# Attention key masks in quarters of the array's rows, those of two score groups together

## Chip, cores and metric

The kernel runs on one core of a Trainium2 chip. The core has a matrix engine (TensorE, PE in the profile, with its weight loads shown apart as PEld), a vector engine (DVE), a scalar engine (ACT), a general engine (POOL) and a queue engine (SP) that issues most transfers. The metric is the device time of one execution in microseconds; the figure used is the median of several runs.

## The reference

The reference is an attention layer followed by a mixture-of-experts feed-forward layer, added to the input. The attention has 16 sequences of 512 tokens and 16 heads of width 64, with one key and value shared by all heads, an additive bias per head, a causal mask and a key mask per sequence. The part that matters here, shortened:

```python
q = (xn @ Wq).reshape(b, n, H, DH).transpose(0, 2, 1, 3) * scale
sim = jnp.einsum('bhid,bjd->bhij', q, k)
sim = sim + bias
sim = jnp.where(causal_mask, neg, sim)
...
sim = jnp.where(mask_p[:, None, None, :], sim, neg)
attn = jax.nn.softmax(sim, axis=-1)
out = jnp.einsum('bhij,bjd->bhid', attn, v)
```

The key mask hides keys of a sequence from all its queries and heads. After attention come a projection, a layer norm, and a layer of 16 experts in which each expert picks its 512 best tokens.

## The kernel before

The attention stage runs over 16 sequences x 8 head pairs = 128 pairs, in one loop over `p` (line 630). A pair is two heads, and its work is spread over several rounds of the loop: in round `p` the scores of pair `p` are computed and reduced, the queries of pair `p + 1` are projected, the probabilities of the pair behind are transposed in squares by DVE and moved by transfers, and the pair behind that one is multiplied with the values (`attend`). Beside this run the output projection of the sequence before (`project`), norms, and the preparation of the sequence after (`turn`, `keys_values`, `turn_values`, `mask`). The order on each engine is the order in which the program is written: the wrapper `Pinned` (line 119) keeps it. Transfers on SP are placed by the scheduler.

The scores of a pair are causal, so the query block `q` of 128 rows has 128 (q + 1) keys: 512, 384, 256 and 128 columns for blocks 3, 2, 1 and 0. They go to PSUM in three groups: block 3, then blocks 2 and 0 in one bank, then block 1. Each group takes two tiles, one for each head, of the pool `ps_s`, which has four. `scores` (line 425) writes them. The two heads of the pair lie in the two halves of the array's 128 rows: head 0 in rows 0 to 63, head 1 in rows 64 to 127, with keys `ka` and queries `qa` laid out accordingly, so that their matmuls run beside each other.

The key mask is added by a matmul of its own ahead of each score product, into the same PSUM tile: the stationary operand `one_sb` is zero but for one row of ones in each half (lines 189 to 192), and the moving operand `km` has, in that row, 0 for a key that counts and -2^100 for one that doesn't. Both are bf16; the score product is fp32. In each call the order is mask, product, mask, product:

```python
te.matmul(
    sps[j][:, at : at + w], one_sb[halves[j], :], sq.km[halves[j], :w],
    start=True, stop=False,
)
```

`mask` (line 270) fills `km` once for each sequence: for each half it loads the 512 mask bytes into a row of `m8` over SP, and DVE converts that row into the row of `km`. There are two `km` tiles, used in turn.

After the scores, `reduce` (line 449) on DVE adds the bias and takes each row's extreme, and frees the PSUM tiles; `exps` on ACT follows. The body of the loop (lines 645 to 670) calls `scores(3)`, `scores(2, 0)`, the reductions of blocks 3, 2 and 0, then two of the four steps of the next pair's queries (half of them), `scores(1)`, the rest of the queries, and the reduction of block 1.

Of the kernel before, what the change touches and what calls it, by code (L numbers as in the profile page):

```python
# [8 lines left out]
F32 = mybir.dt.float32  # L9
# [3 lines left out]
U8 = mybir.dt.uint8  # L13
# [6 lines left out]
P = 128  # L20
# [6 lines left out]
def tile_adaln_ffn(  # L27
# [21 lines left out]
    nc = tc.nc  # L49
    B, N, D = x.shape  # L50
    H = 2 * bias.shape[0]
    DH = null_kv.shape[1]
    E, _, F = fc1.shape
# [14 lines left out]
    ext = [P * (q + 1) for q in range(QB)]  # L68
# [60 lines left out]
    te, ve, se, ge = [Pinned(a) for a in (nc.tensor, nc.vector, nc.scalar, nc.gpsimd)]  # L129


    with ExitStack() as st:
# [3 lines left out]
        small = st.enter_context(tc.tile_pool(name="small", bufs=4))  # L136
# [7 lines left out]
        ps_s = st.enter_context(tc.tile_pool(name="ps_s", bufs=4, space=PSUM))  # L144
# [41 lines left out]
        mhalf = const.tile([P, 1], F32, name="mhalf")  # L186
        nc.vector.memset(mhalf, -0.5)

        one_sb = const.tile([P, P], BF16, name="one_sb")
        nc.vector.memset(one_sb, 0.0)  # L190
        for j in range(2):
            nc.vector.memset(one_sb[j * DH : j * DH + 1, :], 1.0)
        kms = []
        for i in range(2):
            km = const.tile([P, N], BF16, name=f"km{i}")
# [31 lines left out]
        def load_bias(p):  # L227


            bt = biasp.tile([P, 2, SW], F32, name=f"bias_{p}", tag="bias")  # L230
            if p >= HP:
                nc.sync.dma_start(out=bt, in_=causal[p % HP])
                return bt
            nc.sync.dma_start(out=bt, in_=bias[p])
            for q in range(QB):
                diag = bt[:, :, off[q] + ext[q] - P : off[q] + ext[q]]
                ge.affine_select(
                    out=diag, in_=diag, pattern=[[0, 2], [-1, P]],
                    compare_op=ALU.is_ge, fill=-BIG, base=0, channel_multiplier=1,
                )  # L240
            nc.sync.dma_start(out=causal[p], in_=bt)
            return bt

        class Sequence:
# [23 lines left out]
                )  # L268

            def mask(self):  # L270
                m8 = small.tile([DH + 1, N], U8, name=f"m8_{self.b}", tag="m8", bufs=1)
                self.km = kms[self.b % 2]
                for r in (0, DH):
                    nc.sync.dma_start(out=m8[r : r + 1, :], in_=mask[self.b : self.b + 1, :])
                for r in (0, DH):
                    ve.tensor_scalar(
                        self.km[r : r + 1, :], m8[r : r + 1, :], BIG, -BIG, ALU.mult, ALU.add
                    )
# [125 lines left out]
        class Pair:  # L404
# [17 lines left out]
                self.qa = qap.tile([P, N], F32, name=f"qa_{self.name}", tag="qa")  # L422
                se.activation(self.qa, qp, AF.Copy, scale=scale)

            def scores(self, *blocks):

                sq = self.sq
                sps = [
                    ps_s.tile([P, N], F32, name=f"sp_{self.name}_{j}_{blocks[0]}", tag="s")
                    for j in range(2)  # L430
                ]
                halves = [slice(j * DH, (j + 1) * DH) for j in range(2)]
                at = 0
                for q in blocks:
                    w = ext[q]
                    for j in range(2):
                        te.matmul(
                            sps[j][:, at : at + w], one_sb[halves[j], :], sq.km[halves[j], :w],
                            start=True, stop=False,
                        )  # L440
                    for j in range(2):
                        te.matmul(
                            sps[j][:, at : at + w], self.qa[halves[j], q * P : (q + 1) * P],
                            sq.ka[halves[j], :w], start=False, stop=True,
                        )
                    self.sps[q] = [sps[j][:, at : at + w] for j in range(2)]
                    at += w

            def reduce(self, q, bias_t):

# [105 lines left out]
        def steps(*parts):  # L556
            for part in parts:
                if hasattr(part, "__next__"):
                    yield from part
                else:  # L560
                    part()
                yield

        def some(todo, n=None):

            while n is None or n > 0:
                if next(todo, todo) is todo:
                    return
                n = None if n is None else n - 1
# [7 lines left out]
        halves, norms, routes, first, ins, loads = {}, {}, {}, {}, {}, {}  # L577
        early = HP - 3
        for b in range(B):
            at = b * HP  # L580
# [48 lines left out]
        now, behind, turned, late = None, None, None, ()  # L629
        for p in range(B * HP + 1):  # L630
            b, hp = divmod(p, HP)
            now, ahead = ahead, None
            if p + 1 < B * HP:
                biases[p + 1] = load_bias(p + 1)
                ahead = Pair(seqs[(p + 1) // HP], (p + 1) % HP)
            for c, t in loads.get(p, ()):
                seqs[c].load(t)
            bt = biases.pop(p, None)
            chains = [InNorm(seqs[c], t) for c, t in ins.get(p, ())]
            if p in norms:  # L640
                chains.append(OutNorm(seqs[norms[p][0]], norms[p][1]))
            second = steps(*[seqs[c].project(*divmod(h, 2)) for c, h in halves.get(p, ())])
            asked = ahead.queries() if ahead else steps()

            if now:
                now.scores(3)
                now.scores(2, 0)
                now.reduce(3, bt)
                now.exps(3)
                now.reduce(2, bt)  # L650
                now.reduce(0, bt)
                now.exps(2)
                now.exps(0)
            for n in late:
                n.root()
            if now and behind:
                behind.turn()
                behind.move(nc.sync, range(6, SN * SN))
                behind.move(ge, range(6))
            for n in late:  # L660
                n.d()
            some(asked, 1)
            if now:
                now.scores(1)
            else:
                behind.turn_last()
            some(asked)
            if now:
                now.reduce(1, bt)
                now.exps(1)  # L670
            some(second, 1)
            if p in routes:
                seqs[routes[p][0]].turn_router(routes[p][1])
            for n in chains:
                n.a()
            if now:
                now.sums()
            if turned:
                turned.attend()
            for n in chains:  # L680
                n.b()
            if now:
                now.normalize(0)
                now.normalize(3)
            for part in first.get(p, ()):
                part()
            if now:
                now.normalize(2, 1)
            some(second, 2)
            if p in routes:  # L690
                seqs[routes[p][0]].logits(routes[p][1])
            some(second)
            for n in chains:
                n.c()
            late = chains
            for t in {HP - 2: (0,), HP - 1: (1,), HP: (2, 3)}.get(p - end * HP, ()):
                seqs[end].project_part(t, range(early))
            if not now:
                behind.attend()
            turned, behind = behind, now  # L700
# [64 lines left out]
    te, ve, ge = [Pinned(a) for a in (nc.tensor, nc.vector, nc.gpsimd)]  # L765
# [49 lines left out]
    with ExitStack() as st:  # L815
# [107 lines left out]
        groups = []  # L923
# [253 lines left out]
    now = Expert(0, first)  # L1177
# [11 lines left out]
    for e in range(E):  # L1189
# [72 lines left out]
        now = nxt  # L1262
# [53 lines left out]
```

## Time and profile before

| | us |
|---|---|
| median of 3 runs | 3651.52 |
| lowest, highest | 3649.92, 3652.57 |
| the profiled execution | 3655.35 |
| its span in the profile | 3653.6 |
| score products, x2048, first and last start | 50.2 to 1898.1 |
| mask products, x1024, first and last start | 49.5 to 1897.8 |

The profiled execution's span starts with its first and ends with its last recorded instruction, so the execution is 1.75 us longer than it. Attention fills a little over half of the span; the experts follow. In the profile, `sp<-km,one_sb` is a mask product, `sp<-ka,qa` a score product, `qp` a query projection, `op` an output projection, `ap` the product with the values, `xfp` a transpose or a router product, and `p<-sp,bias,nn_sb` on DVE a reduction. Nearly all are recorded at line 127, that of the wrapper, so they are told apart by their tiles. A shape such as 64*128 ahead of the operand sizes is the part of the array that a matmul uses, rows by columns. A time in a line of the timeline is the start of the first instruction in it, and the next number is how long the line's instructions lasted together; matmuls overlap, so the distance between starts tells what one costs.

### The profile page before, as it was taken

To read this page: it belongs to the slowest core of one execution; us is meant where nothing else is said; L and a number is where in the kernel's file an instruction comes from. 1 tells how busy PE (TensorE), PEld (TensorE's weight loads), DVE (VectorE), ACT (ScalarE), POOL (GpSimd) and SP (SyncE) were. 2 spreads that over 40 slices of the span, in tenths; PEclk is the share of its full clock that TensorE was granted. 3 is DMA by queue.
4 is the path that set the end of the run, shared out by engine and by line. 5 is a ranking of instruction groups with operands and counts; after the bars stand their busy time and mean duration, and the time that the engine had idled before them with its cause. 6 is when DMAs were issued, how large, how long until landed. Compare 5 with 4: busy or idle time off the path is not lost.

```text
span 3653.6 us, 52226 instructions
## 1 busy us (share of the span) xinstructions
PE 3441.1 (94%) x16972; PEld 2478.7 (68%) x16972; DVE 2330.9 (64%) x6028; ACT 1585.2 (43%) x4152; POOL 894.3 (24%) x1314
## 2 busy tenths in 40 slices
PE   5799999999999999999993699999999999999998
PEld 2355556555565555555552488888888888888887
DVE  4567676777667767767656865555565666555553
ACT  3567676676666766667660111111121111111111
POOL 2232332332332323233320222111121122222110
PEclk9799999999999999999996799999999999999999
DMA  7777666676667676676642233333333334333330
GB/s 251 241 212 225 207 205 209 211 221 214 203 208 222 213 212 205 205 214 198 196 148 104 70 118 110 104 93 94 115 122 119 119 122 122 110 122 110 112 91 12
DMA packets 263286, 583.58 MB, mean 160 GB/s; under 512 B 49255, under 2 KB 118023, under 8 KB 245607
## 3 DMA queue, kind: packets, MB, share of 16 engines
q1 hardware_dynamic: 215680, 473.44, 39.0%
q0 software_dynamic: 42960, 101.29, 12.3%
q10 hardware_dynamic: 4375, 5.53, 0.4%
q8 instruction: 136, 2.23, 0.3%
q14 instruction: 135, 1.11, 0.1%
HBM read 349.64 MB, written 61.87 MB: 113 GB/s over the span
## 4 chain that ended last, share of the span: by engine, by line
PE 50%; DVE 5%; issue 1%; DMA 1%; POOL 0%; ACT 0%; SPq 0%; DVEq 0%; POOLq 0%; ACTq 0%
PE r_y L127 9%; PE pc L127 6%; PE pc_y L127 6%; PE pa_y L127 6%; PE pa L127 6%; PE pe L127 3%; PE pb L127 3%; PE pd L127 3%; PE op L127 2%; PE qp L127 2%; PE sp L127 1%; PE ap L127 1%; DVE sel L836 1%; PE xgp L127 1%; DVE sq L127 1%
## 5 line engine op out<-in xcount | busy, mean ns | idle before, releaser
L127 ACT ACTIVATE p<-p,nm 128x512 f32<-128x512 f32 (+3 forms) x1024 | 561.9, 550 | 243.8 <-DVE nm L127 242.5
L127 DVE CUSTOM_DVE_ANT_0 p<-sp,bias,nn_sb 128x512 f32<-128x512 f32 (+3 forms) x1024 | 500.5, 546 | 174.1 <-PE sp L127 174.0
L127 POOL DMA_DIRECT2D pt<-sq x762 | 381.6, 508 | 877.6 <-issue 559.8
L127 PE MATMUL qp<-xnt,wq_sb 128*128 128x512 f32 x1024 | 512.2, 623 | 0.0
L127 PE MATMUL op<-wo_sb,ot 128*128 128x256 f32 x1920 | 457.0, 382 | 8.8 <-ACT ot L127 8.6
L127 PEld LDWEIGHTS op<-wo_sb,ot 128*128 128x128 f32 x1920 | 357.4, 190 | 109.3 <-issue 54.3
L127 DVE STREAM_TRANSPOSE sq<-p 128x896 f32<-128x896 f32 x762 | 398.7, 589 | 49.8 <-DMA pt<-sq 27.5
L127 ACT ACTIVATE p<-p,rs 128x512 f32<-128x512 f32 (+2 forms) x768 | 406.2, 603 | 1.9 <-DVE rs L127 1.1
L127 POOL DMA_INDIRECT out_dram<-y,tok x64 | 106.2, 1659 | 1184.3 <-ACT y L1145 1184.3
L1053 ACT ACTIVATE h<-h,b_sb 128x512 f32<-128x512 f32 (+1 forms) x256 | 143.4, 607 | 529.1 <-DVE h L127 471.1
L127 PE MATMUL sp<-ka,qa 64*128 64x512 f32 (+3 forms) x2048 | 357.7, 440 | 1.8 <-ACT qa L127 1.8
L127 PE MATMUL ap<-pt,vp 128*64 128x512 f32 (+3 forms) x2048 | 310.8, 446 | 18.6 <-DMA pt<-sq 9.1
L1145 ACT ACTIVATE y<-y,gg 128x512 f32<-128x512 f32 x64 | 46.2, 722 | 647.3 <-DVE y L127 647.3
L127 PEld LDWEIGHTS qp<-xnt,wq_sb 128*128 128x128 f32 x1024 | 174.9, 190 | 183.2 <-issue 167.8
L127 PEld LDWEIGHTS ap<-pt,vp 128*64 128x64 f32 x2048 | 148.8, 139 | 195.4 <-issue 158.1
L127 PE MATMUL pa<-xe,w 128*128 128x256 f32 x1024 | 243.5, 381 | 0.0
L127 PEld LDWEIGHTS sp<-ka,qa 64*128 64x128 f32 x2048 | 174.2, 190 | 87.5 <-issue 81.5
L127 PE MATMUL pa_y<-w,h 128*128 128x256 f32 x1024 | 231.5, 379 | 0.0
L127 PE MATMUL r_y<-w2t,hs 128*128 128x256 f32 x1024 | 231.5, 379 | 0.0
L127 PEld LDWEIGHTS pa<-xe,w 128*128 128x128 f32 x1024 | 195.9, 191 | 27.0
L127 PEld LDWEIGHTS r_y<-w2t,hs 128*128 128x128 f32 x1024 | 194.6, 190 | 26.5
L127 PEld LDWEIGHTS pa_y<-w,h 128*128 128x128 f32 x1024 | 193.4, 190 | 25.7
(191 smaller groups left out, 5191.6 us busy)
## 6 DMA issues: line engine op xcount, KB each, us to landing
bias<-causal SPq DMA_DIRECT2D x120, 1280.0 KB
w<-in_fc_dram SPq DMA_DIRECT2D x256, 512.0 KB
pt<-sq SPq DMA_DIRECT2D x1270, 80.0 KB
pt<-sq POOLq DMA_DIRECT2D x762, 80.0 KB
x<-in_x_dram SPq DMA_DIRECT2D x64, 256.0 KB
out_dram<-x SPq DMA_DIRECT2D x64, 256.0 KB
table<-xf SPq DMA_DIRECT2D x64, 256.0 KB
bias<-in_bias_dram SPq DMA_DIRECT2D x8, 1280.0 KB
```

Source lines behind the costliest of these rows:

```text
L127: return lambda *args, **kwargs: tc.keep_in_program_order(made(*args, **kwargs))
L836: nc.vector.tensor_scalar(flags, l2, than, None, op, ALU.add, accum_out=red)
L1053: nc.scalar.activation(a[0], a[1], AF.Gelu, bias=b1_sb[:, self.e, f : f + 1])
L1145: nc.scalar.activation(y, y, AF.Copy, scale=self.gg[:, g, self.e : self.e + 1])
```

## The change

The rows of ones and masks stand in four quarters of 32 rows instead of two halves: rows 0, 32, 64 and 96. `mask` loads and converts four rows for each sequence instead of two. `scores` takes groups of blocks. It first writes the masks of all the groups it is given, group 0 in the first quarter of each head's half and group 1 in the second, 32 rows each, and then all the score products, which are 64 rows as before. Blocks 3 and (2, 0) now go together in one call as two groups; block 1 is a call of its own with one group. The flag that clears a bank stands only on the first mask in each bank.

```diff
+        MR = P // 4
         one_sb = const.tile([P, P], BF16, name="one_sb")
         nc.vector.memset(one_sb, 0.0)
-        for j in range(2):
-            nc.vector.memset(one_sb[j * DH : j * DH + 1, :], 1.0)
+        for r in range(0, P, MR):
+            nc.vector.memset(one_sb[r : r + 1, :], 1.0)
...
             def mask(self):
-                m8 = small.tile([DH + 1, N], U8, name=f"m8_{self.b}", tag="m8", bufs=1)
+                m8 = small.tile([P, N], U8, name=f"m8_{self.b}", tag="m8", bufs=1)
                 self.km = kms[self.b % 2]
-                for r in (0, DH):
+                for r in range(0, P, MR):
                     nc.sync.dma_start(out=m8[r : r + 1, :], in_=mask[self.b : self.b + 1, :])
-                for r in (0, DH):
+                for r in range(0, P, MR):
                     ve.tensor_scalar(
                         self.km[r : r + 1, :], m8[r : r + 1, :], BIG, -BIG, ALU.mult, ALU.add
                     )
...
-            def scores(self, *blocks):
+            def scores(self, *groups):
...
+                for g, blocks in enumerate(groups):
+                    sps = [
+                        ps_s.tile([P, N], F32, name=f"sp_{self.name}_{j}_{blocks[0]}", tag="s")
+                        for j in range(2)
+                    ]
+                    at = 0
+                    for q in blocks:
+                        self.sps[q] = [sps[j][:, at : at + ext[q]] for j in range(2)]
+                        at += ext[q]
+                    for q in blocks:
+                        for j in range(2):
+                            rows = slice(j * DH + g * MR, j * DH + (g + 1) * MR)
+                            te.matmul(
+                                self.sps[q][j], one_sb[rows, :], sq.km[rows, : ext[q]],
+                                start=(q == blocks[0]), stop=False, skip_group_check=True,
+                            )
+                for blocks in groups:
+                    for q in blocks:
+                        for j in range(2):
+                            te.matmul(
+                                self.sps[q][j], self.qa[halves[j], q * P : (q + 1) * P],
+                                sq.ka[halves[j], : ext[q]], start=False, stop=True,
+                                skip_group_check=True,
+                            )
...
-                now.scores(3)
-                now.scores(2, 0)
+                now.scores((3,), (2, 0))
...
-                now.scores(1)
+                now.scores((1,))
```

More of the change, by code (lines that the diff above doesn't have):

```diff
@@ L423, in queries @@
                 se.activation(self.qa, qp, AF.Copy, scale=scale)
-            def scores(self, *blocks):
+            def scores(self, *groups):
                 sq = self.sq
[L428 to L431, printed above, removed]
                 halves = [slice(j * DH, (j + 1) * DH) for j in range(2)]
[L433 to L447, printed above, removed]
+                for g, blocks in enumerate(groups):
[22 more added lines that the diff above has]
+                            )
```

## The prediction

> **What bounds the kernel now.** I read the page first, for the busy shares and their course, then the stretches of the attention stage, then the timeline of one head pair, and last the waits of the PE. The change touches only the attention stage, about the first 1.9 ms.
>
> ```profile
> PE 3441.1 (94%) x16972; PEld 2478.7 (68%) x16972; DVE 2330.9 (64%) x6028; ACT 1585.2 (43%) x4152; POOL 894.3 (24%) x1314
> PE   5799999999999999999993699999999999999998
> ```
>
> The reader is to see that the PE row stands at 9 from the fourth slice of 91 us to the end of attention. The stretches say it in microseconds:
>
> ```profile
> 400.00:800.00 400.00, 393.10 (x2070) 232.21 (x2068) 284.11 (x936) 279.29 (x777) 124.19 (x221) 1.00 0.70 214
> 800.00:1200.00 400.00, 393.43 (x2077) 235.38 (x2074) 278.28 (x918) 277.67 (x770) 127.00 (x223) 1.00 0.69 210
> ```
>
> After the two times come PE, weight loads (PEld), DVE, ACT and POOL, then the granted clock. PE is busy 393 of 400 us at full clock; DVE and ACT have 116 us or more free. So what lengthens the PE's own sequence lengthens the stage. Busy time cannot price it, because overlapping matmuls each count; the starts do. One pair, PE alone:
>
> ```profile
> 802.10 1.89 PE L127 MATMUL op<-wo_sb,ot 128*128 128x256 f32 x8
> 803.92 0.39 PE L127 MATMUL sp<-km,one_sb 64*128 64x512 bf16 x2
> 804.15 1.02 PE L127 MATMUL sp<-ka,qa 64*128 64x512 f32 x4
> 805.01 0.33 PE L127 MATMUL sp<-km,one_sb 64*128 64x384 bf16 x2
> 805.17 0.81 PE L127 MATMUL sp<-ka,qa 64*128 64x384 f32 x4
> 805.82 0.22 PE L127 MATMUL sp<-km,one_sb 64*128 64x128 bf16 x2
> 805.87 0.44 PE L127 MATMUL sp<-ka,qa 64*128 64x128 f32 x4
> 806.24 1.98 PE L127 MATMUL qp<-xnt,wq_sb 128*128 128x512 f32 x4
> 808.16 0.28 PE L127 MATMUL sp<-km,one_sb 64*128 64x256 bf16 x2
> 808.28 0.60 PE L127 MATMUL sp<-ka,qa 64*128 64x256 f32 x4
> 808.81 1.98 PE L127 MATMUL qp<-xnt,wq_sb 128*128 128x512 f32 x4
> 810.63 1.89 PE L127 MATMUL op<-wo_sb,ot 128*128 128x256 f32 x8
> 812.35 0.60 PE L127 MATMUL xfp<-ident,xf 128*128 128x128 f32 x4
> ```
>
> Each fp32 product is two passes, so x4 is two heads in two passes. The differences of starts give a mask 0.23, 0.16, 0.05 and 0.12 us (blocks 3, 2, 0, 1; both heads side by side), and the score products 0.86, 0.65, 0.37 and 0.53.
>
> The same lines price a change of the array's shape. Eight output products run 810.63 to 812.35, 1.72 us, when the next uses the same 128 rows; the same eight run 802.10 to 803.92, 1.82 us, when a 64-row matmul follows: **0.10 us for the switch**. Four query passes are 4 x 0.427 = 1.71 us (half of 0.86 per pass, as score block 3 shows for 512 columns). After a switch into 128 rows they take 808.81 to 810.63, 1.82 us, though no switch follows: **0.10 us for a weight load that is not hidden**. With a switch at both ends they take 806.24 to 808.16, 1.92. The weight loads show why:
>
> ```profile
> 804.58 0.10 PEld L127 LDWEIGHTS <-one_sb 64*128 64x128 bf16 x2 [0.24 <-issue]
> 806.24 0.30 PEld L127 LDWEIGHTS qp<-xnt,wq_sb 128*128 128x128 f32 x2
> 808.80 0.30 PEld L127 LDWEIGHTS qp<-xnt,wq_sb 128*128 128x128 f32 x2 [0.33 <-issue]
> ```
>
> Inside one shape the load runs 0.43 us ahead of its matmul (804.58 for the mask at 805.01); across a switch it starts with its matmul. A bf16 load of the ones costs little after a switch: the mask of 512 columns takes 0.23, where half of a pass, 0.213, is its streaming.
>
> **What the Trainium skill says.** "TensorEngine Tiling (Array Packing)", Tiling Modes: changing the tiling mode, not just the tile, drains the TensorE, while different tiles run in parallel. The trace agrees for 128 to 64 rows and back (0.10 us) and for parallel halves; 32 rows occur nowhere in it. The same page, Restrictions and Gotchas: different row tiles must not write one PSUM bank at a time. The change's four quarters write four tiles of their own, so this forbids nothing. "TensorE: Matmul & The Clock Gate", Part 3: four row tiles of 32 rows and 512 columns gained 3.07 times; no run here shows it yet. Its section on LDWEIGHTS prices a load by its 128 columns, not its rows, at columns over 1.2 GHz, about 0.107 us; the trace's exposed 0.10 agrees. So 32-row loads are no cheaper, and a 64-row load is like a 128-row one.
>
> **The change part by part.**
>
> *Masks of blocks 3, 2 and 0.* They now stand ahead of all three products, block 3 in one quarter of each head's half, blocks 2 and 0 in the other. The row lasts as long as block 3, 0.23 us; 0.16 + 0.05 lie beside it (0.213 of streaming in sequence). Removed: 0.21 us.
>
> *Product of block 0.* Before, mask 0 and product 0 take 805.82 to 806.24, 0.42, of which 0.10 is the switch out; the rest, 0.32, is three loads' worth, since a pass of 128 columns is shorter than its load. With the masks gone the first load hides under block 2's last pass (0.32), and two passes of 0.107 remain: 0.21. The mask's 0.05 is counted above, so another 0.06 goes. Removed in this call: 0.27.
>
> *The added switch.* The masks are 32 rows, the products 64. Between them stands a switch the old order did not have: 0.10, and the queries' fp32 weights, which were loaded under the mask, load after it: 0.10. I take the 128/64 price for 32/64; below, it could be 0, if quarters and halves are no different shapes to the array; above, little more than 0.25. Added 0.20; net of this call **-0.07 us**.
>
> *Block 1.* It gets its switch and load too, and nothing goes parallel: its two masks were side by side already. **+0.20 us**.
>
> *Sum.* +0.13 to 0.14 us a pair; 0.135 is taken. There are 128 pairs. The first ten start between 49.5 and 200 us, mostly with 1.6 to 9 us of PE waiting each (their bias comes from outside and is masked and written back); I count them at nothing. 118 x 0.135 = +15.9 us.
>
> *What follows on DVE.* Product 3 ends 0.20 us later after the call's start, so the reductions start 0.20 later. Mostly DVE waits there for PE anyway (1.33 us before the reduction at 805.21). One pair in eight, hp 1, is the exception: DVE is late from the short pair before (9.7 us), and the mask of block 1 waits for its slot:
>
> ```profile
> PE sp L127 <- DVE nm L127: 18.6, 26, 5.3
> PE kp L127 <- ACT ot L127: 13.5, 27, 0.8
> ```
>
> In the 14 later sequences that wait is 0 to 0.8 us. DVE's chain there starts from the pair before, so it moves by 0.20 where PE would have moved by 0.07: 14 x 0.13 = +1.8. The second line's waits follow the PE itself and stay.
>
> *Mask 2 moved ahead of product 3.* It now needs its slot, which the last reduction of the pair before frees, 1.09 us earlier, and product 3 stands behind it in PE's queue. From the eleventh pair on the trace has 1.3 us or more between that reduction and mask 3, so nothing waits. In the early pairs 2, 5 and 9 the reduction ends 0.9 to 2.4 us after mask 3: there product 3 would start up to 1.3 us later. They wait for bias too: 0 to 4 us, taken as 0.
>
> *Preparation.* Two more mask conversions a sequence on DVE at 0.416 us each, 0.83. From the third sequence on DVE idles 0.79 and then 0.99 us right after the old two, which covers them; without that cover 14 x 0.83 = 11.6 us. In the first sequence nothing covers: they stand ahead of the norm (20.42), whose result frees the buffer for the next input load (issued 23.23, right after xn ends at 23.20). +0.8 us once. The two more one-row loads a sequence on SP, 0.30 us of issue each at 31.08, stand ahead of bias and transposed-block moves; SP issues about ten moves of 0.59 us in a pair of 14 us, so it has room. The two small memsets at the start lie under the loads. The clearing flag only once per bank costs nothing.
>
> Sum: 15.9 + 1.8 + 0.8 = **+18.5 us**. Against the profiled execution (3655.35 us: span 3653.6 and 1.75 around it) this is 3673.9; that execution is 3.8 us above the median, so against 3651.52 it is **3670.0**.
>
> **The rivals.**
>
> *No switch price between 32 and 64 rows* (ends faster). The place is the border between the masks and the first product of each call, the price 2c a pair against 0.267 gained: it decides below c = 0.134 us, where I take 0.20. For it: every switch in the trace involves a full-height or a half-width array, none two kinds of row split. Against: both kinds seen cost the same 0.10, and the skill names any mode. At c = 0: -0.267 x 118 + 0.8 = -31 us, 3621.
>
> *The drain costs, the load does not* (c = 0.10): -0.07 x 118 + 0.8, about -7.5, 3644. For it: loads of other row groups can run ahead. Against: at every switch in the trace load and matmul start together.
>
> *The four quarters do not run side by side*, so the change doesn't do what it says: the 0.213 stays and the switches come on top, +0.348 x 118 + 2.6 = +44, 3695. For it: no 32-row work in this trace. Against: the halves overlap to within 4 ns of start.
>
> **How the numbers follow.** My case 0.67; no switch price 0.12; drain without load 0.12; quarters in a row 0.09. My case alone is 3662 to 3679 (c from 0.18 to 0.22 is +-5 us, early pairs +4, noise). The range 3641 to 3688 takes in the drain without load and the near part of quarters in a row, and leaves out about 0.18. A measurement of this kernel can tell 0.2%, 7.3 us, from no change. Slower: 0.65 of my case and most of the last, 0.73. Within: half of the drain-only case and a rest of mine, 0.08. Faster: 0.19.
>
> **What would show it.** Right: masks 3 and 2 starting within some 10 ns of each other, mask 3 to product 3 about 0.43 us, mask 0 inside that time, mask 1 to product 1 about 0.2 with a first pass longer by 0.1, first call 2.25 us, pairs longer by 0.13. The load of the queries' weights should start with product 3. Wrong: that load starting with the masks (no switch), or mask 2 starting 0.2 us after mask 3 (no overlap), or new PE waits for DVE at masks from the eleventh pair on.

## The result, and the profile after

The median of the changed kernel is 3671.99 us (six runs, 3668.97 to 3677.9) against 3651.20 us before (six runs): ratio 1.0059, interval 1.0046 to 1.0072. The change costs about 21 us. The prediction said 3670.0, in a range of 3641 to 3688.

The page and the stretches of the kernel after, the lines that answer to those of before:

```profile
PE 3459.3 (94%) x16972; PEld 2480.3 (68%) x16972; DVE 2344.2 (64%) x6062; ACT 1588.4 (43%) x4152; POOL 894.0 (24%) x1314
PE   5799999999999999999994499999999999999998
```

```profile
400.00:800.00 400.00, 391.65 (x2050) 230.52 (x2050) 281.64 (x928) 276.35 (x765) 125.04 (x222) 1.00 0.69 210
800.00:1200.00 400.00, 391.64 (x2038) 231.61 (x2035) 279.19 (x917) 272.55 (x758) 122.83 (x216) 1.00 0.68 209
```

The PE is as full as before and does fewer instructions in the same 400 us (2050 against 2070): the stage runs slower at an unchanged share of busy time. So the share tells nothing here, and the starts must. The timeline of the PE, the same pair (sequence 6, hp 4) as in the prediction:

```profile
812.35 0.40 PE L127 MATMUL sp<-km,one_sb 32*128 32x512 bf16 x6
812.68 2.00 PE L127 MATMUL sp<-ka,qa 64*128 64x512 f32 x12
814.61 1.98 PE L127 MATMUL qp<-xnt,wq_sb 128*128 128x512 f32 x4
816.52 0.28 PE L127 MATMUL sp<-km,one_sb 32*128 32x256 bf16 x2
816.73 0.70 PE L127 MATMUL sp<-ka,qa 64*128 64x256 f32 x4
817.37 1.98 PE L127 MATMUL qp<-xnt,wq_sb 128*128 128x512 f32 x4
```

All six masks take 0.33 us to the first product, the switch included: they do run side by side. In the trace's single records the four masks of blocks 3 and 2 start within 10 ns. The first call, 812.35 to 814.61, takes 2.26 us (2.32 before); block 1, 816.52 to 817.37, takes 0.85 (0.65 before). The weight loads show the switch, first the load of the queries (`qa`) for block 3 before, then the loads after:

```profile
803.93 0.41 PEld L127 LDWEIGHTS sp<-ka,qa 64*128 64x128 f32 x4
```

```profile
812.35 0.12 PEld L127 LDWEIGHTS <-one_sb 32*128 32x128 bf16 x6 [0.33 <-issue]
812.68 0.30 PEld L127 LDWEIGHTS sp<-ka,qa 64*128 64x128 f32 x4 [0.21 <-ACT p L127]
816.73 0.30 PEld L127 LDWEIGHTS sp<-ka,qa 64*128 64x128 f32 x4
```

The load of the queries starts with its product, at 812.68 and again at 816.73, where before it started with the mask (803.92), 0.22 us ahead of its product. So the price has two parts: 0.10 us at the border between 32 and 64 rows (mask to product takes 0.33 instead of 0.23), and 0.10 us of a load that nothing hides (the product's first pass takes 0.53 instead of 0.43). The wait for ACT named at 812.68 is not the reason: at 816.73 no wait is named, and the load starts with its product all the same. The waits of the PE (microseconds in all, times, longest), first that of the output products (`op`) for ACT before, then the lines after:

```profile
PE op L127 <- ACT ot L127: 8.6, 12, 1.7
```

```profile
PE sp L127 <- DVE nm L127: 23.1, 28, 5.6
PE kp L127 <- ACT ot L127: 13.7, 27, 0.8
PE op L127 <- ACT ot L127: 10.1, 11, 1.6
```

The masks' wait for DVE grew from 18.6 to 23.1 us, but most of that lies in the first ten pairs. From the eleventh pair on it went from 4.4 to 6.1 us, 15 times in both: 1.7 us, about what the prediction gave to hp 1.

The starts of the first mask in each pair give the length of a pair. After against before, pairs 11 to 119 (median of a group; for hp 1, which varies, the mean): +0.13 us in hp 0, 2, 3 and 5, **+0.20 in hp 4, 6 and 7**, +0.37 in hp 1. A sequence of eight gains 4 x 0.13 + 3 x 0.20 + 0.37 = 1.5 us, times 14.75 sequences 22 us. The last pair starts 22.3 us later than before.

Hp 1's 0.37 has two parts. Up to its last eight output products (`op`) the pair grew from 11.90 to 12.15 us, 0.25. These products grew from 2.61 to 2.74 us, but they contain a wait for ACT's `ot` that differs by some 0.4 to 0.5 us (standard deviation) between the sequences of one profile; with the order of before (e1_rows, below) they take 2.84. So 0.12 a sequence, 1.8 of the 22 us, is not shown to come from the change.

Why hp 4, 6 and 7 lose more shows in the timeline of one such pair, hp 6 of sequence 14, at the transpose for the router (`xfp`). It reads `xf`, the rows that DVE writes as the last step of a norm begun in the round before. First before, then after:

```profile
1766.05 0.71 DVE L127 SCALAR_TENSOR_TENSOR xf<-z,rms_r,nw_sb 128x512 f32<-128x512 f32 x1
1767.11 0.60 PE L127 MATMUL xfp<-ident,xf 128*128 128x128 f32 x4
1767.67 1.08 PE L127 MATMUL ap<-pt,vp 128*64 128x512 f32 x4
```

```profile
1787.42 0.71 DVE L127 SCALAR_TENSOR_TENSOR xf<-z,rms_r,nw_sb 128x512 f32<-128x512 f32 x1
1788.40 0.60 PE L127 MATMUL xfp<-ident,xf 128*128 128x128 f32 x4
1789.04 1.08 PE L127 MATMUL ap<-pt,vp 128*64 128x512 f32 x4
```

In both, `ap` starts 0.91 us after DVE has finished `xf` (1766.76 to 1767.67, 1788.13 to 1789.04). From `xfp` to `ap` it is 0.56 before and 0.64 after. The trace's records of the PE's queue, which the timeline leaves out, fill the 0.91: the wait for `xf` goes through at 1788.17, and behind it stand seven records of waits for two semaphores each, from 1788.29 to 1788.93, one about every 0.107 us, ahead of `ap`, which reads what the transfers brought. Before, the same seven stand from 1766.92 to 1767.56. While the queue stands at `xf`, those waits do not run ahead. DVE reaches `xf` along a chain that starts with the reduction of block 3: reductions of 3, 2, 0, six square transposes, `xf`. So in hp 4, 6 and 7 it is the end of block 3's product that sets the time, and that end moved by 0.20 us, not 0.13. (The fourth router transpose stands in hp 2 of the next sequence and reads an `xf` written a round earlier; hp 2 loses 0.13.) Before, the two limits lay within 0.04 us of each other, as the runs with an early `xf` below show, and so nothing stood out.

### The profile page after: what moved, and what is told of

Read it like the earlier page. It is cut to its first block, busy times and chain, and to the rows that moved or that the text cites. A ratio compares the mean times of both kernels' runs of the same rounds, so it can differ in the third digit from the quotient of the medians.

```text
span 3669.9 us, 52283 instructions
## 1 busy us (share of the span) xinstructions
PE 3459.3 (94%) x16972; PEld 2480.3 (68%) x16972; DVE 2344.2 (64%) x6062; ACT 1588.4 (43%) x4152; POOL 894.0 (24%) x1314
## 4 chain that ended last, share of the span: by engine, by line
PE 50%; DVE 4%; DMA 1%; issue 1%; SPq 0%; POOL 0%; ACT 0%; POOLq 0%; DVEq 0%; ACTq 0%
PE r_y L127 9%; PE pa L127 6%; PE pc L127 6%; PE pc_y L127 6%; PE pa_y L127 6%; PE pd L127 3%; PE pe L127 3%; PE pb L127 3%; PE op L127 2%; PE qp L127 1%; PE sp L127 1%; DVE sel L842 1%; PE ap L127 1%; PE xgp L127 1%; DVE sq L127 1%
## 5 line engine op out<-in xcount | busy, mean ns | idle before, releaser
L127 PE MATMUL sp<-ka,qa 64*128 64x512 f32 (+3 forms) x2048 | 349.1, 459 | 0.7 <-ACT qa L127 0.7
```

The costliest lines, as they stand in the source:

```text
L127: return lambda *args, **kwargs: tc.keep_in_program_order(made(*args, **kwargs))
```

## The experiments

Theory P: the PE's own sequence decides, as nearly all of the prediction's sum had it. Theory D: besides it, the end of block 3's product decides in hp 4, 6, 7 (through `xf`) and hp 1 (through the PSUM slot). Each run is given against the kernel before on the same chip.

**Block 1 alone in quarters** (e2_block1).

```diff
-                now.scores(1)
+                now.scores(1, rows=P // 4)      # mask of 32 rows; the rest as before
```

> The kernel before, with one part of the change: only the mask of block 1 is 32 rows high, the masks of blocks 3, 2 and 0 stay in halves and in the old order. Theory P (what counts is the PE's own sequence, 0.07 us saved in the first call and 0.19 us lost in the second): +0.19 x 118 = +22 us, about 3674, more than the whole change. Theory D (besides the PE's sequence, the moment at which block 3's product ends counts, since DVE's chain starts from it and in the pairs with a router transpose decides when the PE goes on): the same here, +22, since block 3's product does not move.

Measured: 3667.36 against 3651.70, ratio 1.0046 (1.0030 to 1.0061), +15.7 us. The pairs show +0.20 in hp 2, 3, 5, +0.16 in hp 4, 6, 7, and 0.22 in hp 0 and 1 together. The price of one switch with its load is as reckoned; the expected 22 was too high, because the PE's old waits for DVE in hp 1 and in the router pairs take a part of it (the masks' waits from the eleventh pair on fall from 4.4 to 0.4 us).

**The first call alone in quarters** (e3_first).

```diff
                             rows = slice(j * DH + g * MR, j * DH + (g + 1) * MR)
+                            if len(groups) == 1:
+                                rows = halves[j]
```

> The changed kernel with block 1's masks back in halves (64 rows; both rows of ones of a half count there, so a masked key of block 1 gets -2^101 instead of -2^100). The quarters are left in the first call alone, where the PE's sequence is shorter by 0.06 us a pair but block 3's product ends 0.20 us later. Theory P: -0.06 x 118 + 0.8 = -7 us, about 3645. Theory D: the three pairs in eight with a router transpose after a full DVE chain (hp 4, 6, 7) lose 0.20 each, hp 1 some 0.3, the other four gain 0.06: +0.65 a sequence x 14.75, about +9 us, 3660.

Measured: 3664.22, ratio 1.0036 (1.0022 to 1.0049), +12.5 us. The pairs: -0.06 in hp 2, 3, 5, where the call is indeed shorter; +0.20 in hp 4, 6, 7; +0.46 in hp 0 and 1 together. Theory P, which expected -7, falls. The part of the change that shortens the PE's sequence costs 12.5 us by itself. (Of the 0.46, 0.28 lies in hp 1's scattering wait for `ot`.) The two parts, 15.7 and 12.5, add up to more than the whole 21: where block 3's delay of 0.20 already decides, block 1's 0.20 partly falls into the same wait.

**The order of the change, without a 32-row matmul** (e5_halves).

```diff
-                            rows = slice(j * DH + g * MR, j * DH + (g + 1) * MR)
+                            rows = halves[j]
```

(and two rows of masks instead of four).

> No 32-row matmul at all: the order of the change (masks of blocks 3, 2, 0, then the three products), but each mask in the halves, 64 rows, one after the other. No switch is added, and the PE's sequence of the call is as long as before (0.05 exposed load of block 3 against 0.055 saved at block 0), but block 3's product ends about 0.26 us later. Theory P: no change, 3651. Theory D: hp 4, 6, 7 lose 0.26 each and hp 1 some 0.3 to 0.4: about 1.1 a sequence x 14.75 = +16 us, 3667.

Measured: 3665.90, ratio 1.0048 (1.0034 to 1.0061), +14.2 us. The PE's timeline of the same pair:

```profile
809.74 0.61 PE L127 MATMUL sp<-km,one_sb 64*128 64x512 bf16 x6
810.18 1.94 PE L127 MATMUL sp<-ka,qa 64*128 64x512 f32 x12
812.06 1.99 PE L127 MATMUL qp<-xnt,wq_sb 128*128 128x512 f32 x4
```

The call takes 2.32 us, the same as before, and no load waits for a switch. Still hp 4, 6 and 7 lose 0.27 each and hp 1 0.28, hp 0, 2, 3 and 5 nothing. A delay of block 3 alone, at no cost to the PE, gives the loss: theory D.

**The same, with `xf` taken out of the way** (e5d_halves_early). The late norm's last step moves ahead of four of the six square transposes:

```diff
-                behind.turn()
+                behind.turn(late)               # calls n.d() after its first two transposes
```

> The kernel of e5_halves, and besides it the last step of the late norm on DVE (xf) moved ahead of four of the six square transposes that stood before it, so that the router transpose's input is ready about 1.3 us earlier. Theory D: the loss in hp 4, 6, 7 goes (0.26 x 3 x 14.75 = 11.5 us), the one in hp 1 stays or grows a little: about 3656. Theory P: as e5_halves, whatever that is; if e5_halves loses for another reason (mask 2 waiting for its PSUM slot, or the masks themselves), the loss stays at about +16.

Measured: 3654.65, ratio 1.0009 (1.0001 to 1.0017), +3.0 us. In hp 4, 6 and 7 the pairs now are 0.035 shorter than before, in hp 0 and 1 together they keep 0.26. The timeline of hp 4:

```profile
811.65 0.70 DVE L127 SCALAR_TENSOR_TENSOR xf<-z,rms_r,nw_sb 128x512 f32<-128x512 f32 x1
813.46 0.60 PE L127 MATMUL xfp<-ident,xf 128*128 128x128 f32 x4
813.99 1.08 PE L127 MATMUL ap<-pt,vp 128*64 128x512 f32 x4
```

`xf` is done at 812.35, over 1 us ahead of its transpose, and from `xfp` to `ap` it is 0.53 us. The seven waits in the PE's queue now go through from 812.52 to 813.16, all ahead of the transpose at 813.46. With that, the wait behind most of e5_halves's loss is shown, and mask 2 waiting for its slot is ruled out, since that order is the same in both.

**Both kinds of quarters with `xf` early**: the edit above in e3_first's kernel (e3d_first_early) and in the changed kernel (a_early, second).

> The kernel of e3_first (quarters in the first call alone, block 1 in halves) with the late norm's last step moved ahead of four transposes. Theory D: in hp 4, 6, 7 block 3's later end no longer decides, so these pairs gain 0.06 and the 0.04 that they waited before, -0.10 each, hp 2, 3, 5 keep -0.06, hp 0 and 1 together keep about +0.4: -0.1 a sequence x 14.75 = about -1 us against the kernel before, no change within 0.2%. Without theory D it stays at e3_first's +12.5.

Measured: 3651.34 against 3650.85, ratio 0.9999 (0.9991 to 1.0008). The pairs: -0.06 (hp 2, 3, 5), -0.10 (hp 4, 6, 7), +0.64 in hp 0 and 1 together, where +0.4 was expected. The 12.5 us of e3_first are gone, and nothing is won either: what the six other pairs gain, hp 1 gives back (0.24 of its 0.71 lies in the wait that scatters).

> The changed kernel with the same move. Theory D: hp 4, 6, 7 fall from +0.20 to +0.13 - 0.04 = +0.09, the rest stays: 3 x 0.11 x 14.75 = 4.9 us less than the change, about +16 against the kernel before (ratio about 1.0044).

Measured: 3669.54, ratio 1.0050 (1.0037 to 1.0064), +18.7 us. Hp 4, 6 and 7 go from +0.20 to +0.095. The difference from the change's 21 lies inside the intervals; the traces carry it, with the last pair 17.8 us later than before instead of 22.3.

**The preparation alone** (e1_rows: four mask rows loaded and converted, two of them without ones against them):

```diff
-                for r in (0, DH):
+                for r in range(0, P, P // 4):
```

> The kernel before with the change's preparation alone: four mask rows loaded and converted for each sequence, though only the old two have ones against them. If DVE's idle time right after the conversions covers the two new ones, +0.8 us once at the start, about 3652.5. If it does not, up to 0.83 x 14 = 11.6 us more, 3663.

Measured: 3657.22 against 3656.50 on another chip, ratio 1.0004 (0.9996 to 1.0013): no change that can be told; 11.6 us are excluded. Hp 4, where the conversions stand, is as long as before. Hp 1 is 0.23 longer in the mean, all of it in its last output products, though their order and the PE's are untouched: that is the scatter of two profiles.

**Both groups in one quarter** (e4_one_quarter), so that they cannot lie side by side:

```diff
-                            rows = slice(j * DH + g * MR, j * DH + (g + 1) * MR)
+                            rows = slice(j * DH, j * DH + MR)
```

> The changed kernel with the masks of both groups in the same quarter of each head's half, so that blocks 3, 2 and 0 cannot lie beside each other; shapes, switches and order stay. If the quarters of the changed kernel do run side by side, this takes that away: first call +0.21 against the change, block 3's product 0.41 later than before. By theory D 0.34 in hp 2, 3, 5, 0.41 in hp 4, 6, 7, 0.6 in hp 0 and 1 together: 2.85 a sequence x 14.75 = +42 against the kernel before, about 3693. By theory P 0.34 x 118 = +40, 3692. If the quarters bring nothing, 3672 as the change.

Measured: 3699.52, ratio 1.0118 (1.0102 to 1.0133), +43 us. The PE's timeline of hp 4:

```profile
821.04 0.61 PE L127 MATMUL sp<-km,one_sb 32*128 32x512 bf16 x6
821.58 2.00 PE L127 MATMUL sp<-ka,qa 64*128 64x512 f32 x12
```

The masks now take 0.54 us to the first product where the change takes 0.33: the 0.21 us that the quarters hide are real. P and D lie too close here to be told apart, as expected.

**Every mask 32 rows high, old order** (e7_each): `scores` of before with 32 rows of mask in every call.

> The kernel before, old order, with every mask 32 rows high in the first quarter of its half: four switches from 32 to 64 rows a pair (0.20 each with the exposed load) and two from 64 back to 32 (0.11), less 0.055 at block 0: +0.77 in the first call, +0.19 in the second. 0.96 a pair in most, some 1.5 in hp 0 and 1 together: about 7.1 a sequence x 14.75 = +105 us, 3756. If the price belonged to the pair of calls and not to each switch, it would be near the change's +21.

Measured: 3751.64, ratio 1.0262 (1.0246 to 1.0278), +95 us. The timeline of hp 4:

```profile
836.88 0.39 PE L127 MATMUL sp<-km,one_sb 32*128 32x512 bf16 x2
837.20 1.13 PE L127 MATMUL sp<-ka,qa 64*128 64x512 f32 x4
838.26 0.34 PE L127 MATMUL sp<-km,one_sb 32*128 32x384 bf16 x2
838.53 0.92 PE L127 MATMUL sp<-ka,qa 64*128 64x384 f32 x4
839.38 0.23 PE L127 MATMUL sp<-km,one_sb 32*128 32x128 bf16 x2
839.53 0.49 PE L127 MATMUL sp<-ka,qa 64*128 64x128 f32 x4
```

Mask and product of block 3 take 1.38 us (836.88 to 838.26) against 1.09 before: 0.20 for going into 64 rows, its bare load included, and 0.09 for going back. The price belongs to each switch, in both directions. The pairs show 0.95 as reckoned; hp 0 and 1 together lose 0.84, not the expected 1.5, so hp 1's wait hides more than I had taken, and this is the missing 10 us.

**A version without quarters** (e8d_small_first): block 0's mask ahead of block 2's and both ahead of their products, and `xf` early.

```diff
-                for q in blocks:
+                for q in reversed(blocks):
...
-                            start=True, stop=False,
+                            start=(q == blocks[-1]), stop=False, skip_group_check=True,
```

(the products follow in a loop of their own).

> A version without quarters: the kernel before, with block 0's mask ahead of block 2's and both ahead of their products (all 64 rows; block 0's weights then load under block 2's last pass), and the late norm's last step moved ahead of four transposes as in e5d_halves_early. Block 3's product does not move. Theory D: -0.055 in hp 2, 3, 5, -0.095 in hp 4, 6, 7, nothing in hp 0 and 1: -0.45 a sequence x 14.75 = -6.6 us, about 3645. Theory P: -0.055 x 118 = -6.5, the same, so this run is not to tell them apart but to see whether a version beats both kernels.

Measured: 3649.45 against 3656.50, ratio 0.9982 (0.9975 to 0.9989). It beats the kernel before by about 7 us, where 6.6 was expected (3645 was reckoned from another chip's median), and so the changed one too, though that one was not run on this chip. The pairs: -0.055 (hp 2, 3, 5), -0.09 (hp 4, 6, 7), and +0.09 in hp 0 and 1 together, where nothing was expected; what costs it there was not followed up. Its call:

```profile
803.05 0.39 PE L127 MATMUL sp<-km,one_sb 64*128 64x512 bf16 x2
803.27 1.02 PE L127 MATMUL sp<-ka,qa 64*128 64x512 f32 x4
804.13 0.38 PE L127 MATMUL sp<-km,one_sb 64*128 64x128 bf16 x4
804.35 1.03 PE L127 MATMUL sp<-ka,qa 64*128 64x384 f32 x8
805.31 1.98 PE L127 MATMUL qp<-xnt,wq_sb 128*128 128x512 f32 x4
```

It takes 2.26 us, as short as the change's, with block 3 as early as before and no switch. So the 0.06 us by which the change shortens that call is no more than what putting block 0's mask ahead brings, where it frees block 0 of a bare weight load; the 0.21 of the quarters are eaten up by the 0.20 of the switch.

## Why the prediction was right, point by point

- *The switch between 32 and 64 rows costs what 128/64 costs, 0.20 with the load.* Right: block 1 went from 0.65 to 0.85 us, and e7_each repeats it per switch. The sentence of the Trainium skill ("TensorEngine Tiling (Array Packing)", Tiling Modes) that a change of mode drains the TensorE holds here between 32 and 64 rows too, at 0.10 us. The rivals without the whole price are out: in the lines above no load ran ahead over this border.
- *The quarters run side by side.* Right: 0.21 us lies between the change and e4_one_quarter.
- *First call -0.07.* Right: 2.32 to 2.26. A pass of 128 columns was called shorter than its load; block 0's two passes after start 0.109 us apart, so pass and load are about alike, and the sum stands. One sign that I named was wrong in its place: I gave mask 3 to product 3 as 0.43 us. It is 0.33; the exposed load shows in the length of the product's first pass instead, 0.53 us between the starts of its passes against 0.43 before. The sum is not touched.
- *+0.135 a pair in 118 pairs.* Right in hp 0, 2, 3 and 5. **The mis-sized term** is "What follows on DVE": it said that DVE mostly waits for the PE anyway and counted hp 1 as the one exception, at 0.13 a sequence. For hp 1 that was right: 0.25 apart from the scattering wait, against 0.135 + 0.13. But hp 4, 6 and 7 lost 0.07 more each, through `xf`, which the prediction did not name: 3 x 0.07 x 14.75, about 3 us. The sign that it named for being wrong, new waits for DVE at masks, could not show this, since the wait stands at the router transpose. That DVE stood idle before the reduction did not show slack for what came a dozen operations later in its queue.
- *The first ten pairs at nothing.* Right as far as can be told: the eleventh started 0.8 us earlier than before, and in the profiles of the other runs it lies between 1.8 us earlier and 1.4 later. With it go the 0 to 4 us of mask 2 ahead of product 3, rightly taken as 0. (The 1.3 us of room given from the eleventh pair on holds in all pairs but one of the last sequence, with 0.94.)
- *+0.8 us at the start.* Wrong, and small. The first norm on DVE did begin 0.59 us later (21.01 against 20.42), though not for the conversions' own time alone: DVE waited 1.71 us for the load of a mask row. The next tile's load was issued later (23.60 against 23.23), but the norm that reads it still began at 29.39 (29.41 before), and the first mask started at 49.18 instead of 49.5. In none of the profiles with four rows does it start later than before. The lateness did not carry through that load, which I had taken to pass it on.
- *The other mask conversions are covered.* Right, by e1_rows.

The sum, +18.5, missed 3 us in hp 4, 6 and 7 and had 0.8 too many at the start; that these two errors have opposite signs is luck. With both put right it is about 20.7, against the 20.8 between the medians, nearer than the interval (17 to 26 us) can tell.

## What to carry to other kernels

Packing matmuls into smaller row tiles pays when what lies side by side is worth more than entering and leaving the mode: here 0.20 us a call (0.10 at the border and 0.10 of an fp32 weight load that nothing hides), against 0.21 saved in one call and nothing in the other. Read that price in the trace of before, from the same instructions with and without a neighbour of another shape. And when a change moves a result later inside a stage that is bound by one engine, follow the consumer's queue to the next place where the bound engine waits for it, however idle the consumer looks where it receives the result.

## What was not expected of the hardware

- Ahead of an instruction that waits for many semaphores, the PE's queue here held a record for each pair of them, about 0.107 us apart (seven from 1788.29 to 1788.93 in the kernel after), and with an unfinished wait ahead of them none ran early. Where `xf` was early, all seven ran ahead of the transpose (812.52 to 813.16 in e5d_halves_early). This turned a late `xf` into a late `ap`.
- A round of one expert takes mostly either 98.45 us or about 99.05 (the first 103.5 or 104.1): seven of the fifteen rounds were long by 0.6 us in the profile of before, none in that of after, and twelve in that of e8d_small_first, whose chip has many in the other profiles too. That is up to 7 us which no edit to attention explains. The spans of the two profiles differ by 16.3 us while the last pair differs by 22.3; the long rounds make up 4.1 of these 6 us, and 1.9 were made up between the last pair and the first round. What causes the long rounds was not tried.
